# Local attention in 64x32 tiles of the TensorE array instead of 64x64, with queries and keys fetched in another layout

## The chip, the cores and the metric

The kernel runs on one core of a Trainium2 chip. A core has five engines that run their own instruction streams and meet through semaphores: TensorE (PE in the profile; its weight loads are listed apart, as PEld), VectorE (DVE), ScalarE (ACT), GpSimd (POOL) and SyncE (SP), which here does nothing but issue DMAs. TensorE is an array of 128 by 128 cells that can be split into smaller tiles, each with its own stationary operand, its own moving operand and its own place in PSUM. Everything is fp32.

The metric is device time in microseconds of one execution, as the median of several runs. Lower is better.

## The reference

The input is x of 8 batches, 512 tokens, 256 features. It is layer-normed, and two branches start from the result. One is a plain causal attention with one head of 256. The other is a small transformer of two layers, each with local attention and a gated feed-forward part; its output goes through silu and gates the first branch, and x is added. What matters here is the local attention: 8 heads of 64, and windows of 128 queries, each of which sees its own window and the one before.

```python
qkv = h @ wqkv                              # h: tokens, half of the features shifted by one token
q = l2norm(q) * qs;  k = l2norm(k) * ksc
q, k = rotary_xpos(q, k)
# 128 queries (window w) against the 256 keys of windows w-1 and w
sim = jnp.einsum('bhwid,bhwjd->bhwij', bq, bk)
mask = (i < j) | (i > j + WINDOW) | (j == -1)
attn = softmax(where(mask, -max, sim))
out = jnp.einsum('bhwij,bhwjd->bhwid', attn, bv)
x = x + out @ wo
h = layernorm(shift_token(x));  a, g = split(h @ w1 + b1)
x = x + (a * gelu(g)) @ w2 + b2
```

A query with place r in its window may see the keys from place r of the window before to place r of its own: 129 keys.

## The kernel before, in words

The whole program is written as a set of jobs (Python generators), and a string of letters, ORDER, says which job goes on next. A letter stands for a job: A output projections (all_outs), B weighted sums of the values (all_sums), C the attention weights fetched back (p_in), D scores (all_scores), E queries and keys fetched back (turns_in), F the projections to q, k and v, G the late weight loads (late_loads); H and later letters are the first branch, the feed-forward parts and the ends of single batches. TensorE's instructions stand in exactly this order. For the other engines and for SP a planner (class Order) keeps a time line with estimated costs, puts every instruction into the first gap that fits and keeps that order in the program. The planner's estimates are used for the order alone; TensorE, DVE, ACT, POOL and SP each run their instructions strictly one after another, and an instruction that waits holds up those behind it.

The work is done in 16 slots, a slot being one layer of one batch, and in 4 steps t of 128 tokens in each slot: 64 steps. In a step:

- F (project): q, k and v of 128 tokens, three pairs of matmuls of 512 columns on the full array. ACT, DVE and POOL square, rotate and normalise q and k.
- turn_out: q and k are turned by 32x32 blocks on DVE (rt) and sent to DRAM (away) by four DMAs.
- E (turns_in): they come back with features on partitions: k in one DMA (kT, 256 KB), q in four DMAs of 64 KB each (qT), which write pieces of 32 numbers, 128 bytes, so that the 64 queries of a half window lie side by side. There are three buffers for kT, of one step each, and one for qT; a step's keys stay for the next step.
- D (all_scores): for each half g of the heads, 64 queries at a time against the keys that they can see, in tiles of 64 rows (features of one head) by 64 columns (queries); four such tiles fill the array. Two rows of heads (a) times two halves of the window (h) run side by side. The two halves of the window see 192 keys each: 128 in a first matmul and 64 in a second. In step t = 0 there is no window before, and 128 keys are used. DVE adds the mask and takes the greatest (192 columns a head), ACT makes the exponentials and sums, DVE the reciprocals, and either scales.
- p_out: DVE turns the weights by 32x32 blocks (pr), and eight DMAs (four for t = 0) send them to DRAM (p_away).
- C (p_in): two DMAs fetch them back with keys on partitions (pT), three slots of 64 keys.
- B (all_sums): values by weights, in tiles of 64 rows (keys) by 64 columns (features of a head). For each pair of heads (c), matmuls of 128 columns and of 64 columns (queries) write two PSUM banks, which are then added into oT.
- A (all_outs): output projection.

matmul (line 297) tells the planner what a matmul costs: its columns, divided by the number of tiles side by side. `order.CHANGE` holds what the planner reckons for a change of the array's split. All DMAs are issued on SP: load for inputs and weights, send for the rest. late_loads issues the weights of the first layer's feed-forward part and then those of the second layer, a few at a time.

Of the kernel before, what the change touches and what calls it, by code (L numbers as in the profile page):

```python
# [15 lines left out]
P = 128  # L16
BATCH = 8
T = 512
# [11 lines left out]
WINDOW = 128  # L30
EPS = 1e-5
# [11 lines left out]
    "H6JFH2FHFGHF3JHE3NF2HEH3FHFH2FENH2D2HJCE2CJCFJF2EGD2FJGEJ2GEDCDBECEFJC2JFJF2JBEFD2JF2C2E"  # L43
    "GCAEFJ2ABC2FIJFEFEGJ2FJ2GDBDJCN3FENCIAFAI2CNENFIEBDN2FDNIENFNCNIRE2I2C2I3BD2NICEINCFNF3"
    "D2E2NFCAF2EAKNCNBRCNKEKER2CRDRF2BFRDC2AEAFRKDR2EF3EFK2RCF2RDER2CFBEDCDFKRECE2KEKCDBDCFE"
    "F2ACARCRFE2BD2RC2KF2CFLFBCFECK2A2EDLDCEBCECLKF3ELKDF4LRBEDLRF2CE2ACAEFD2FCLECL2D2BFCECFE"
    "FEFCOL2BLACAEDODO2EF2ECFLCF2OEBCDCLF2MFDMECOBEME2FO2CMFD2MAECFAFEO2CBVD2F2C2OFE2FOBFECPF"
    "RC2FD2VAVECEPVFOE2AVPBPC2V2FOPDBFDFEF2CPVDCDCAECEPFVPVFEPFVABDCVEF2CVEFVFDEBFPED2C2E2VPC"
    "PFAF3CFVABE2S2DSCSFPCFPQBDESEQ2FSQCV2CA2D2EC2STVQFEF2ES2DBEDVZSCEFVFCSF2SBD2ZFAEFACFEFST"
    "CE2TCZ2TZ3SBD2C2F2EFCEFZCZBCD2FEFCFAZCTAFZBZTCEFTEZCWEF2TFD2BFCZE2T2ETATAED2WZWFWEWF2CET"  # L50
    "CZ2CTDWBCEDECF4U2CBUFEFWC2WUFA2D2CBCXCUFW2ZFEF3EdWEWZBD2ZECE2FWZCADCDFdAEF2XCWBXdXEdECd2"
    "CFd2EDFBDdEFCXFAXDCDAEFEFCFdECXFX3BCD2aEF3ECdFEXEBD2dCFdF2EdEdXAaC2aCAF2XDFDBC2dadXBEC2E"
    "dEYF2EdECFY2AaADFBDY2bFaC2aFahE2CEFaFaF2BD2CdFEA2aFCECFahbED2b2adhFbCEah2F3D2EBh2Cb2ECEb"
    "FbBDECEC2DFAhCFEAF2BDECDFbEFEeFCbFBbCe2AEACED2eF2ECFCF2bhD2FBC2ebBFECF2AFCECEeEhFEeAFD2C"
    "EBEeCF2ehCEFD2fFEe3EBfD2hCcCF2cAC2AhEfFeBEfCFCeDBDFfFfFC2FE2CcEhEFEA2fDcDf2EF2fFD2CBECh"
    "F2CFfBFCEfEi2FiEFAC2AhiEfBDiDFECF2fCiCDEDciE2i3gi2DBDiCiFCACFAFjgFCjBE2CFCFjFEFBFhA2jE2h"
    "jDhF2DEFhFhD2CgF2jgjC2jEjECEBC2gjED2ECjBCEjFA2l2D2Clj2lkBklC2kl2Cl2klBlA2n2knl2n2m3o2n7o"
    "no"
# [19 lines left out]
class Order:  # L78
# [9 lines left out]
        "full": {"rows": 0.193, "columns": 0.148, "quarters": 0.148},  # L88
        "rows": {"full": 0.196, "columns": 0.142, "quarters": 0.142},
        "columns": {"full": 0.209, "rows": 0.2, "quarters": 0.155},  # L90
        "quarters": {"full": 0.22, "rows": 0.2, "columns": 0.165},
# [150 lines left out]
def gated_attention_kernel(  # L242
# [28 lines left out]
    counts |= {"st": 2, "p0": 2, "p": 6, "pr": 1, "pT": 2, "qT": 1, "kT": 3, "v": 4, "sq": 2, "side": 2}  # L271
# [25 lines left out]
    def matmul(out, lhsT, rhs, start, stop, shape="full"):  # L297
        columns = max(out.free_size(), lhsT.free_size())
        side_by_side = {"full": 1, "rows": 2, "columns": 2, "quarters": 4}[shape]
        order.took((columns * 4 / 2400 * 1.0055 + 0.01 * (shape == "quarters")) / side_by_side, shape)  # L300
        nc.tensor.matmul(out, lhsT=lhsT, rhs=rhs, start=start, stop=stop)  # L301
# [63 lines left out]
    mask_sb = const.tile([P, T + 2 * P], F32, tag="mask", name="mask_sb")  # L365
# [50 lines left out]
    window_mask = mask_sb[:, T + DH : T + 2 * P]  # L416
# [321 lines left out]
    def turns_in():  # L738


        for b, l, t in steps:
            yield {"after": [event("parked", b, l, t)]}
            away, at = parked.pop((b, l, t))
            yield {"free": {"kT": 1}}
            dst = buffer("kT", [P, INNER], f"kT_{b}_{l}_{t}")
            there = send(dst, away[P : 2 * P], at, LAND[256])
            kTs[b, l, t] = dst.rearrange("p (s c b) -> p s c b", s=4, c=IC)
            done("kT", b, l, t, at=there)
            yield {"free": {"qT": 1}}
            dst = buffer("qT", [P, INNER], f"qT_{b}_{l}_{t}")  # L750
            parts = dst.rearrange("p (h c s b) -> h s p c b", h=2, c=IC, s=2)
            for s in range(4):
                src = away[0:P, s * P : (s + 1) * P].rearrange("p (c b) -> p c b", c=IC)
                there = send(parts[s // 2, s % 2], src, at, LAND[64])
            qTs[b, l, t] = dst.rearrange("p (h c n) -> p h c n", h=2, c=IC)
            done("qT", b, l, t, at=there)

    steps = [(b, l, t) for b, l in slots for t in range(NT)]

    def late_loads():  # L760


        yield {"after": [event("asked", 1)]}
        for some in behind_x:
# [21 lines left out]
    main = slice(0, P), slice(P + DH, 2 * P + DH)  # L786
    rest = slice(P, P + DH), slice(2 * P + DH, 3 * P)
    oTs = {}

    def all_scores():  # L790
# [4 lines left out]
        for b, l, t in steps:  # L795
            nm = f"{b}_{l}_{t}"
            n = P if t == 0 else P + DH
            used = main if t == 0 else (slice(0, P + DH), slice(P + DH, 3 * P))
# [4 lines left out]
            for g in range(2):  # L803
# [6 lines left out]
                qT, kT, before = qTs[b, l, t], kTs[b, l, t], kTs.get((b, l, t - 1))  # L810
                sps = [bank(f"sps_{nm}_{g}_{a}") for a in range(2)]
                blocks = [(main, ((before or kT, slice(0, 4)), (kT, slice(0, 4))))]
                if t > 0:
                    blocks.append((rest, ((kT, slice(0, 2)), (before, slice(2, 4)))))
                for columns, keys in blocks:
                    for i in range(2):
                        c = 2 * g + i
                        for a, rows in enumerate(halves):
                            for h, (tile_, some) in enumerate(keys):
                                matmul(  # L820
                                    sps[a][halves[h], columns[i]],
                                    qT[rows, h, c],
                                    tile_[rows, some, c],
                                    True,
                                    True,
                                    "quarters",
                                )
                if g == 1:
                    free(f"qT_{nm}")
                    if t > 0:  # L830
                        free(f"kT_{b}_{l}_{t - 1}")
                    if t == NT - 1:
                        free(f"kT_{nm}")
                ps = []
                for a in range(2):
                    ends = 0.0
                    p = buffer("p", [P, 3 * P], f"p_{nm}_{g}_{a}")
# [42 lines left out]
    def p_out(ps, g, t, key):  # L880
# [5 lines left out]
        few = 4 if t == 0 else 6  # L886
        if g == 0:
            p_leaving[key], there = claimed("pr", [P, 6, HEADS, 32], f"pr_{nm}")
# [3 lines left out]
        for a, (p, at, name) in enumerate(ps):  # L892

            src = p.rearrange("p (h k a) -> p h k a", h=2, k=6)[:, :, 0:few]
# [7 lines left out]
        away = dram.tile([P, 6, 2 * P], F32, tag="p_away", name=f"p_away_{nm}", bufs=8)  # L902
        rows = away.rearrange("(g a) (s q) n -> a g s q n", g=4, q=2)
        for s in range(4):
# [4 lines left out]
            elif s < 2:  # L909
                parts = [((0, 4), 0, 0), ((4, 6), 1, 0)]  # L910
            else:
                parts = [((0, 4), 2, 0), ((4, 6), 1, 2)]
# [6 lines left out]

    p_leaving, pTs = {}, {}  # L920

# [13 lines left out]
    def all_sums():  # L935


        for b, l, t in steps:
# [12 lines left out]
            for c in range(IC):  # L951

                turned = pT[c // 2]
                two = [
                    (halves[a], slice((2 * c + a) * DH, (2 * c + a + 1) * DH), 2 * a + c % 2)
                    for a in range(2)
                ]
                if t == 0:

                    for on, h, to in two:  # L960
                        matmul(o_ps[0][on, c], v[low, h], turned[low, 0:2, :, to], True, True, "quarters")
# [407 lines left out]
```

## Time and profile before

| | |
|---|---|
| median of 3 runs | 1317.12 us (1316.83 to 1318.29) |
| span of the profiled execution | 1320.0 us |
| TensorE (PE) busy | 1292.7 us, 98%, 10498 records |
| weight loads (PEld) busy | 750.0 us, 57% |
| VectorE (DVE) busy | 1030.6 us, 78% |
| ScalarE (ACT) busy | 751.5 us, 57% |
| GpSimd (POOL) busy | 624.5 us, 47% |
| scores, "sps" | 3584 records, 102.2 us busy |
| DMA | 209.49 MB in 396884 packets, mean 159 GB/s |
| packets under 512 bytes | 153880 |

The page gives the profiled execution's span, from the first to the last of its instructions, and no other time of its own. The span is 2.9 us above the median of the runs shown. A record in the profile is one instruction as the engine ran it; an fp32 matmul on the array leaves two records with a weight load each, a transpose one. "Busy" is the union of the records of a group, so that matmuls that run side by side count once, while their mean durations overlap. "Idle before" is time in which the engine had nothing to do ahead of such a record, and the name behind the arrow is what ended it. In names, "sps" are the score banks, "ops" those of the weighted sums, qkv the projections, qT, kT and pT the turned queries, keys and weights, away and p_away the places in DRAM.

### The profile page before, as it was taken

The page shows a single profiled execution, that of the slowest core. Times are in us where ns is not written, and L with a number is a line of the kernel's source. Part 1 is how long each engine was busy: PE and PEld are TensorE (multiplying, and loading weights), DVE is VectorE, ACT ScalarE, POOL GpSimd, SP SyncE. Part 2 cuts the span into 40 slices and gives each one's busy share as a digit, 9 for nine tenths or more (in the row PEclk, how much of TensorE's full clock was granted, in tenths as well). Part 3 has the DMA queues.
Part 4 walks back from the last instruction along what each step waited for, and adds up shares of the span by engine and source line. Part 5 has one row for each costly group of instructions (what it writes and reads, how often), then busy time and mean ns, then how long its engine had stood idle before and what let it go on. Part 6 is the DMA issues. An engine that isn't in the chain of part 4 may idle for free.

```text
span 1320.0 us, 29777 instructions
## 1 busy us (share of the span) xinstructions
PE 1292.7 (98%) x10498; PEld 750.0 (57%) x10498; DVE 1030.6 (78%) x3088; ACT 751.5 (57%) x1958; POOL 624.5 (47%) x651
## 2 busy tenths in 40 slices
PE   9899999999999999999999999999999999999998
PEld 4565565555555565555655555555455555545566
DVE  6977678778778888888777787878878788866864
ACT  2553554754667376574555547655455647662853
POOL 6746336456353644454625445545454644425500
PEclk9999999999999999999999999999999999999999
DMA  7777435765667656666647666566666766645761
GB/s 250 200 189 211 135 94 144 200 150 141 167 164 202 160 131 153 174 162 145 173 104 188 149 156 156 137 181 157 148 152 157 165 159 170 153 113 145 196 165 56
DMA packets 396884, 209.49 MB, mean 159 GB/s; under 512 B 153880, under 2 KB 382400, under 8 KB 396736
## 3 DMA queue, kind: packets, MB, share of 16 engines
q1 hardware_dynamic: 396736, 207.59, 62.1%
q8 instruction: 84, 1.38, 0.4%
q14 instruction: 64, 0.52, 0.1%
HBM read 111.56 MB, written 95.94 MB: 157 GB/s over the span
## 4 chain that ended last, share of the span: by engine, by line
PE 85%; DMA 5%; DVE 3%; SPq 2%; ACT 2%; issue 1%; POOL 1%; DVEq 0%; ACTq 0%; POOLq 0%
PE qkv L301 22%; PE ff L301 20%; PE w2p L301 12%; PE wop L301 7%; PE sps L301 6%; PE ops L301 6%; PE qk L301 3%; SPq L71 2%; PE sc L301 2%; DMA qT<-away 2%; PE av L301 2%; PE v0p L301 2%; PE hps L305 1%; DMA x<-in_x_dram 1%; DMA pT<-p_away 1%
## 5 line engine op out<-in xcount | busy, mean ns | idle before, releaser
L71 POOL TENSOR_TENSOR r<-r,side 128x512 f32<-128x512 f32 x128 | 163.7, 1279 | 428.9 <-DVE side L71 428.6
L301 PE MATMUL qkv<-wqkv,xT 128*128 128x512 f32 x768 | 354.7, 596 | 0.7 <-ACT pT L71 0.7
L301 PE MATMUL ff<-hn,w 128*128 128x512 f32 (+1 forms) x680 | 283.7, 568 | 1.0 <-ACT hn L71 1.0
L71 ACT ACTIVATE p<-p,nmx 128x192 f32<-128x192 f32 (+1 forms) x512 | 219.4, 429 | 83.6 <-DVE nmx L71 82.9
L301 PEld LDWEIGHTS qkv<-wqkv,xT 128*128 128x128 f32 x768 | 141.1, 190 | 142.4 <-issue 129.3
L71 POOL TENSOR_TENSOR rn<-ss,neg_half 128x8 f32<-128x8 f32 x128 | 212.9, 1663 | 10.7
L301 PEld LDWEIGHTS ff<-hn,w 128*128 128x128 f32 x680 | 128.2, 190 | 139.5 <-issue 124.6
L71 DVE CUSTOM_DVE_ANT_0 p<-sps,mask_sb 128x192 f32<-128x192 f32 (+1 forms) x512 | 146.3, 332 | 21.5 <-PE sps L301 21.4
L301 PE MATMUL w2p<-hid,w 128*128 128x512 f32 (+3 forms) x408 | 160.0, 576 | 0.0
L71 ACT ACTIVATE p<-p,rden 128x192 f32<-128x192 f32 (+1 forms) x283 | 118.5, 433 | 40.5 <-DVE rden L71 39.5
L71 DVE STREAM_TRANSPOSE pr<-p 128x384 f32<-128x384 f32 (+1 forms) x256 | 127.7, 526 | 17.8 <-ACT p L71 14.2
L71 POOL TENSOR_TENSOR r<-r,rn 128x512 f32<-128x512 f32 x128 | 133.6, 1044 | 10.0
L71 ACT ACTIVATE sq<-qkv 128x512 f32<-128x512 f32 x128 | 75.0, 592 | 100.0 <-PE qkv L301 90.7
L71 ACT ACT_TABLE_LOAD x99 | 127.0, 1283 | 2.5 <-PEq L1359 0.7
L71 DVE SCALAR_TENSOR_TENSOR hid<-ff,vec,hid 128x512 f32<-128x512 f32 (+3 forms) x119 | 83.3, 711 | 47.5 <-ACT hid L71 26.2
L301 PE MATMUL wop<-oT,wo 128*128 128x256 f32 x512 | 118.6, 380 | 0.5 <-DVE oT L71 0.5
L301 PEld LDWEIGHTS w2p<-hid,w 128*128 128x128 f32 (+1 forms) x408 | 68.8, 189 | 81.2 <-issue 78.3
L71 DVE TENSOR_TENSOR r<-qkv,tables 128x512 f32<-128x512 f32 x128 | 86.9, 679 | 34.3 <-ACT sq L71 29.2
L301 PE MATMUL sps<-kT,qT 64*64 64x128 f32 (+1 forms) x3584 | 102.2, 253 | 10.6 <-DMA qT<-away 10.0
L301 PEld LDWEIGHTS sps<-kT,qT 64*64 64x64 f32 x3584 | 88.3, 135 | 42.2 <-issue 25.4
L301 PEld LDWEIGHTS wop<-oT,wo 128*128 128x128 f32 x512 | 96.0, 190 | 25.6 <-issue 9.3
L71 DVE STREAM_TRANSPOSE rt<-r 128x512 f32<-128x512 f32 x128 | 90.1, 704 | 18.5 <-POOL r L71 14.0
(83 smaller groups left out, 1679.2 us busy)
## 6 DMA issues: line engine op xcount, KB each, us to landing
pT<-p_away SPq DMA_DIRECT2D x96, 384.0 KB, 4.4
away<-rt SPq DMA_DIRECT2D x256, 128.0 KB, 2.6
p_away<-pr SPq DMA_DIRECT2D x256, 128.0 KB, 2.3
kT<-away SPq DMA_DIRECT2D x64, 256.0 KB, 3.0
qT<-away SPq DMA_DIRECT2D x256, 64.0 KB, 2.9
p_away<-pr SPq DMA_DIRECT2D x192, 64.0 KB, 2.0
pT<-p_away SPq DMA_DIRECT2D x32, 256.0 KB, 3.4
hn_away<-hn SPq DMA_DIRECT2D x60, 128.0 KB, 2.5
```

The lines of the kernel that those rows point to most:

```text
L71: ins = getattr(self.engine, name)(*args, **kwargs)
L301: nc.tensor.matmul(out, lhsT=lhsT, rhs=rhs, start=start, stop=stop)
L305: nc.tensor.transpose(out, in_, ident)
```

## The change

Scores: 32 queries instead of 64 per tile. A block of 32 queries sees 160 keys (SEEN), its own block and the four before it, so that one matmul of 160 columns does what took one of 128 and one of 64 for 64 queries. Tiles are 64 rows by 32 columns, eight fill the array. The weights for a head take 160 columns instead of 192 in the mask, the exponentials, the scaling and the turning.

So that the 160 keys lie in one stretch, each kT buffer now holds the keys of the step before and of its own, side by side. For t > 0 the earlier keys are fetched again from DRAM. There are two such buffers instead of three of half the size. The queries come back in one DMA of whole rows.

Sums: the values' matmuls, of the same columns as before, are split into 32 features each, so that they too use 64x32 tiles; there are twice as many. The weights still come back as three slots of 64 keys. Where a block of 32 queries doesn't see a block of 32 keys of its slot, nothing is written any more; those places have to be zero. So the eight DRAM buffers for t > 0 are now fixed ones, taken in turn, and clear_p_aways writes zeros into these places once, with 32 DMAs of 32 rows by 256 numbers, ahead of the first layer's feed-forward weights on SP.

ORDER, the order of all jobs, is a new string throughout (left out below).

```diff
+BLOCK = 32
+SEEN = WINDOW + BLOCK
...
-    counts |= {"st": 2, "p0": 2, "p": 6, "pr": 1, "pT": 2, "qT": 1, "kT": 3, "v": 4, "sq": 2, "side": 2}
+    counts |= {"st": 2, "p0": 2, "p": 6, "pr": 1, "pT": 2, "qT": 1, "kT": 2, "v": 4, "sq": 2, "side": 2}
...
-        side_by_side = {"full": 1, "rows": 2, "columns": 2, "quarters": 4}[shape]
-        order.took((columns * 4 / 2400 * 1.0055 + 0.01 * (shape == "quarters")) / side_by_side, shape)
+        side_by_side = {"full": 1, "rows": 2, "columns": 2, "quarters": 4, "eighths": 8}[shape]
+        order.took((columns * 4 / 2400 * 1.0055 + 0.01 * (side_by_side > 2)) / side_by_side, shape)
...
             yield {"free": {"kT": 1}}
-            dst = buffer("kT", [P, INNER], f"kT_{b}_{l}_{t}")
-            there = send(dst, away[P : 2 * P], at, LAND[256])
-            kTs[b, l, t] = dst.rearrange("p (s c b) -> p s c b", s=4, c=IC)
+            dst = buffer("kT", [P, 2, INNER], f"kT_{b}_{l}_{t}")
+            if t > 0:
+                send(dst[:, 0], keys_of[b, l, t - 1], 0.0, LAND[256])
+            keys_of[b, l, t] = away[P : 2 * P]
+            there = send(dst[:, 1], keys_of[b, l, t], at, LAND[256])
+            kTs[b, l, t] = dst.rearrange("p t (s c b) -> p (t s) c b", s=4, c=IC)
             done("kT", b, l, t, at=there)
             yield {"free": {"qT": 1}}
             dst = buffer("qT", [P, INNER], f"qT_{b}_{l}_{t}")
-            parts = dst.rearrange("p (h c s b) -> h s p c b", h=2, c=IC, s=2)
-            for s in range(4):
-                src = away[0:P, s * P : (s + 1) * P].rearrange("p (c b) -> p c b", c=IC)
-                there = send(parts[s // 2, s % 2], src, at, LAND[64])
-            qTs[b, l, t] = dst.rearrange("p (h c n) -> p h c n", h=2, c=IC)
+            there = send(dst, away[0:P], at, LAND[256])
+            qTs[b, l, t] = dst.rearrange("p (s c b) -> p s c b", s=4, c=IC)
...
         yield {"after": [event("asked", 1)]}
+        clear_p_aways()
         for some in behind_x:
             some()
...
-                blocks = [(main, ((before or kT, slice(0, 4)), (kT, slice(0, 4))))]
-                if t > 0:
-                    blocks.append((rest, ((kT, slice(0, 2)), (before, slice(2, 4)))))
-                for columns, keys in blocks:
-                    for i in range(2):
-                        c = 2 * g + i
-                        for a, rows in enumerate(halves):
-                            for h, (tile_, some) in enumerate(keys):
-                                matmul(
-                                    sps[a][halves[h], columns[i]],
-                                    qT[rows, h, c],
-                                    tile_[rows, some, c],
...
+                for i in range(2):
+                    for a, rows in enumerate(halves):
+                        for q in range(4):
+                            seen = slice(4, 8) if t == 0 else slice(q, q + 5)
+                            matmul(
+                                sps[a][q * BLOCK : (q + 1) * BLOCK, used[i]],
+                                qT[rows, q, 2 * g + i],
+                                kT[rows, seen, 2 * g + i],
+                                True,
+                                True,
+                                "eighths",
+                            )
...
-            elif s < 2:
-                parts = [((0, 4), 0, 0), ((4, 6), 1, 0)]
             else:
-                parts = [((0, 4), 2, 0), ((4, 6), 1, 2)]
+                own = 4 - s
+                parts = [((0, own), s // 2, s), ((own, 5), 1 + s // 2, 0)]
...
+    p_aways = [
+        dram.tile([P, 6, 2 * P], F32, tag=f"p_away{n}", name=f"p_away{n}", bufs=1) for n in range(1, 9)
+    ]
+
+    def clear_p_aways():
+
+        for away in p_aways:
+            for g, slot, q in ((0, 0, 1), (2, 1, 1), (1, 1, 0), (3, 2, 0)):
+                send(rows_of(away)[:, g, slot, q], mask_sb[0:BLOCK, 0 : 2 * P], arrived["mask"], 2.0)
...
-                two = [
-                    (halves[a], slice((2 * c + a) * DH, (2 * c + a + 1) * DH), 2 * a + c % 2)
-                    for a in range(2)
+                four = [
+                    (
+                        slice(n * BLOCK, (n + 1) * BLOCK),
+                        slice(c * P + n * BLOCK, c * P + (n + 1) * BLOCK),
+                        n // 2 * 2 + c % 2,
+                    )
+                    for n in range(4)
                 ]
...
-                for on, h, to in two:
+                for on, h, to in four:
                     for ps, own, tile_, at in ((o_ps[0], low, v, 1), (o_ps[1], up, before, 0)):
                         columns = turned[own, at : at + 2, :, to]
-                        matmul(ps[on, c], tile_[own, h], columns, True, False, "quarters")
-                for on, h, to in two:
+                        matmul(ps[on, c], tile_[own, h], columns, True, False, "eighths")
+                for on, h, to in four:
                     for ps, own, tile_, at in ((o_ps[0], low, before, 0), (o_ps[1], up, v, 2)):
                         columns = turned[own, at, :, to]
-                        matmul(ps[on, c, own], tile_[own, h], columns, False, True, "quarters")
+                        matmul(ps[on, c, own], tile_[own, h], columns, False, True, "eighths")
...
+    row, col = np.arange(P)[:, None] % BLOCK, np.arange(SEEN)[None, :]
+    window = np.where((col >= row) & (col <= row + WINDOW), f(0.0), f(NEG))
```

## The prediction

> **What bounds the kernel now.** First the page's head, the busy shares and the chain that ended last:
>
> ```profile
> span 1320.0 us, 29777 instructions
> ...
> PE 1292.7 (98%) x10498; PEld 750.0 (57%) x10498; DVE 1030.6 (78%) x3088; ACT 751.5 (57%) x1958; POOL 624.5 (47%) x651
> ...
> PE 85%; DMA 5%; DVE 3%; SPq 2%; ACT 2%; issue 1%; POOL 1%; DVEq 0%; ACTq 0%; POOLq 0%
> ```
>
> TensorE has work almost all the time, so only its own time and its few waits can move the end. DVE, at 78%, matters only where TensorE waits for it. So I read TensorE's groups of instructions (shapes kept apart) for the two that change; the columns are records, busy us, mean ns of one, idle us before them:
>
> ```profile
> L301 PE MATMUL ops<-pT,v 64*64 64x128 f32 x1792 | 87.7, 275 | 4.3 <-DMA pT<-p_away 3.5 <-DVE nmx L71 0.8
> L301 PE MATMUL sps<-kT,qT 64*64 64x128 f32 x2048 | 86.8, 277 | 10.6 <-DMA qT<-away 10.0 <-issue 0.2
> L301 PE MATMUL ops<-pT,v 64*64 64x64 f32 x1792 | 70.0, 220 | 0.0
> L301 PE MATMUL sps<-kT,qT 64*64 64x64 f32 x1536 | 43.9, 220 | 0.0
> ```
>
> Means overlap, since four tiles run abreast; costs must come from starts. Each fp32 matmul leaves two records (the program has 1792 of each kind). The timeline of TensorE (start, length, records):
>
> ```profile
> 108.01 0.67 PE L301 MATMUL sps<-kT,qT 64*64 64x128 f32 x16
> ...
> 312.86 1.46 PE L301 MATMUL av<-v,pT 128*128 128x256 f32 x6
> 314.25 1.57 PE L301 MATMUL ops<-pT,v 64*64 64x128 f32 x64
> ...
> 327.93 10.46 PE L301 MATMUL ff<-hn,w 128*128 128x512 f32 x24
> ```
>
> Full array: 24 records of 512 columns give (10.46 - 0.593)/23 = 0.429 us from start to start; 6 of 256 give (1.46 - 0.38)/5 = 0.216. That is 0.83 ns a column plus 3 ns, so 109 ns for 128 columns, 56 for 64 and 136 for 160. Four abreast: "ops" has 32 records of 128 and 32 of 64, 8 rounds of four each: 8 x 109 + 7 x 56 + 220 for the last one + about 70 to get under way = 1.55 us, against 1.57 shown. So a round of four costs what one matmul of its width costs on the full array. In the single records, neighbours in a round start 7 ns apart.
>
> The waits, with the queue (SPq) that serves them; the last line is the median us from issue to landing:
>
> ```profile
> PE sps L301 <- DMA qT<-away: 10.0, 8, 5.8
> ...
> 58.12 0.51 SPq L71 DMA_DIRECT2D wqkv<-in_wqkv_dram  x1
> 58.69 6.38 SPq L71 DMA_DIRECT2D qT<-away  x4
> ...
> qT<-away SPq DMA_DIRECT2D x256, 64.0 KB, 2.9
> ```
>
> TensorE waits 10.0 us for queries in 8 places; 5.8 of it is one wait that ends at 68.5 us, behind the 1.5 MB weight load issued at 58.12.
>
> **The change, part by part.** Durations are from the profiled execution; its span, 1320.0, is all that the page gives of its time, 2.9 us above the median, 1317.12. The sum is a difference, and I take it off the median.
>
> *Scores.* 48 of 64 steps have t > 0. Before, such a step has 8 rounds of 128 columns and 8 of 64: 8 x (109 + 56) = 1.32 us. After, its 32 matmuls leave 64 records of 160 columns, 8 rounds of eight: 8 x 136 = 1.09 us. 48 x 0.23 = **-11.1 us**, if eight run abreast as four do. The 16 steps with t = 0 keep 8 rounds of 128 columns.
>
> *Sums.* The matmuls double (1792 to 3584) and so do the places: 8 rounds of 128 and 8 of 64 a step, **0** by columns. That holds only if twice the instructions can be issued in the same time.
>
> *A round of eight.* No row has one. From below: no dearer than a round of four. From above: in today's 64-column rounds 4 matmuls and 4 weight loads start in 56 ns, 7 ns each; were that the fastest, eight abreast would take 112 ns whatever the width below 128, and a step of sums (8 + 8 rounds) 1.79 instead of 1.32, +22.6 us over 48. After the wait that ends at 324.6, however, pairs of weight load and matmul start 7 ns apart, half of that price, so 8 pairs fit into 56 ns, just. I take 2 ns a round (64-column rounds today stand 56 to 58 apart): 512 rounds of scores and 896 of sums, **+2.8 us** (0 to +22.6). *Stagger:* the eighth tile starts 7 x 7 = 49 ns after the first, the fourth today 21; each stretch of small tiles ends 28 ns later. The order of the changed kernel as built has 99 stretches: **+2.7 us**. *Turning the array:* today there are 94 stretches; going in costs 522 ns where 429 is the rule, coming out 148 instead of 56, so 5 more cost 5 x 0.185 = **+0.9 us**.
>
> [...]
>
> *The transfers.* Queries come in one DMA instead of four, keys in two instead of one: three issues a step, not five, at about 0.5 us each on SP (the row above: 64 KB, 2.9 us; keys 256 KB, 3.0 us). So the last part arrives about 1 us sooner. The keys have two buffers of twice the size, and the next step's are still fetched while this one's are used; the repeated keys have long been in DRAM. The attention weights still leave in eight issues a step with t > 0, with a sixth fewer bytes. Of the seven shorter query waits, 10.0 - 5.8 = 4.2 us, I take half away: **-2** (-4 to +3). The long one stays behind the weight load, but now with about 9 us of TensorE work after the previous scores instead of 8.4, and two issues less: **-2** (-5.8 to +3).
>
> *Clearing.* 32 transfers of 32 KB are put on SP ahead of the first layer's feed-forward weights. At 0.5 us each that is 16 us. SP stands idle from 19.1 to 27.3 and from 27.7 to 31.7 us today, which covers 12, so the first turned keys leave about 4 us late. Today's first queries are issued until 38.4, land 2.9 us later, by about 41, and are used at 44.25; in the new order the scores come 1.4 us sooner (two groups of transposes moved behind). 4 + 1.4 - 3.3 = **+2 us** (0 to +8: 1.9 MB of weights now go just ahead of them in the same queue). What else waits behind the clears, the third batch's input, isn't needed until about 52 us.
>
> *Off the path.* Masks, exponentials, scaling and transposes shrink from 192 to 160 columns a head: 384 masks at 1 ns a column are 13 us less DVE, and ACT loses some 10. Both lie beside TensorE; they only make its waits for DVE and ACT rarer, and I count nothing. The new order of all stages may add or remove single waits; today's waits for anything but queries come to 1320.0 - 1292.7 - 10.0 = 17 us in all, and I allow a quarter of that, 4 us, to either side.
>
> Sum: -11.1 + 2.8 + 2.7 + 0.9 - 2 - 2 + 2 = **-6.7 us**; 1317.1 - 6.7 = 1310.4, faster by 0.5%.
>
> **The rivals.**
> *Only four abreast.* If the array, or what feeds it, carries four streams of fp32 and not eight, every round of eight takes two: +1.09 us for each of 48 steps of scores and +1.32 for sums, and +0.87 for each of 16 first steps in both: 48 x 2.41 + 16 x 1.74 = 143 us, about 1454. For it: no row shows more than two tiles side by side over the same rows. Against: these two cost nothing over one (109 ns both).
> *Issue is the limit (the other side).* In the sums 128 pairs must go out in 1.32 us, 10.3 ns a pair; at 14 ns, today's rate in 64-column rounds, +22.6 instead of +2.8 ends at 1330. It decides from 11.8 ns a pair on, where the sums lose the 9.5 us that the rest of the sum gains. Fetching instructions works alike: queue q8 brings 16 KB packets, 84 of them, which take 0.9 to 1.8 us in the trace and hold 256 instructions each (21500 of TensorE in all); a stretch of sums and scores now takes 384 in 2.4 us, and some 30 stretches could each stand still for up to 0.5 us, +15 us. Against both: 7 ns a pair after a wait.
> *Other waits take the gain.* The early transfers at their upper bound (+8) and the re-made order at +4 give -6.7 + 6 + 4 = +3, so 1315 to 1321. For it: a slow first stage shifts all that follows. Against: TensorE's waits are few.
>
> **How the numbers follow.** Measurement tells from no change what exceeds about 0.2%, 2.6 us. As forecast 0.64 (1302 to 1315, most at 1310; 0.60 of it faster); issue or fetch 0.13 (1317 to 1335); only four, or rounds much longer, 0.10 (1350 up); other waits 0.13 (1312 to 1322; faster 0.03, same 0.05, slower 0.05). Faster 0.63; same 0.04 + 0.05 + 0.01 = 0.10; slower 0.05 + 0.12 + 0.10 = 0.27. The range has to reach into the slower cases: 1301 (waits of DMA nearly gone as well) to 1333; the likeliest case alone is 1302 to 1315.
>
> **What would show it.** Rounds: 64 records of 160-column "sps" in about 1.4 us, 128 records of "ops" in about 1.6; if these stretches are over 2 us, issue or feeding is the limit. Waits: "sps" for queries below 7 us in sum; a wait before the first "sps" near 42 us of about 2 us. Packets of under 512 B fall by the 131072 of 128 bytes. I am wrong if TensorE's starts in a round of eight are not 7 ns apart, or if the feed-forward's first weights come late because of the clears.

## The result, and the profile after

| | before | after |
|---|---|---|
| median | 1317.07 us (1316.83 to 1318.29) | 1357.04 us (1355.24 to 1361.33, 4 runs) |
| ratio | | 1.0304, 95% interval 1.0285 to 1.0322 |
| profiled span | 1320.0 us | 1353.2 us |

The change makes the kernel 3.0% slower; 0.5% faster was forecast, and 1357.04 lies above the upper end of the range, 1333. The page of the changed kernel, the lines that answer to those shown of before:

```profile
span 1353.2 us, 37815 instructions
...
PE 1306.0 (97%) x14594; PEld 746.8 (55%) x14594; DVE 1003.0 (74%) x3085; ACT 741.0 (55%) x1962; POOL 625.5 (46%) x651
...
DMA packets 273267, 217.29 MB, mean 161 GB/s; under 512 B 21016, under 2 KB 244416, under 8 KB 273088
...
q8 instruction: 116, 1.90, 0.6%
...
PE 87%; DMA 6%; DVE 2%; issue 2%; POOL 2%; SPq 1%; ACT 1%; DVEq 0%; ACTq 0%
```

TensorE still bounds the kernel, but it is idle for 47 us of its span and not for 27, and the chain holds 2% of "issue", time in which the engine waited for nothing that the profile shows. While TensorE works, the granted clock is 0.5 for 13.7 us of this trace and for 6.8 us of the one before. A full-array record of 512 columns takes 854 ns from start to start at 0.5 (at 47 us of this trace), where it takes 429 at 1.00, so that is worth at most 3.4 us of the difference. DVE has 28 us less to do, above all as masks and transposes are narrower. Small packets fell by 132864. Instruction packets rose from 84 to 116: 32 more packets of 256 instructions, that is the 8192 that TensorE has more (4096 records with a weight load each).

TensorE's groups by shape, and its waits (waited for, us in all, times, longest):

```profile
L304 PE MATMUL ops<-pT,v 64*32 64x128 f32 x3584 | 104.7, 279 | 3.3 <-DMA pT<-p_away 1.9 <-DVE hid L73 1.2
L304 PE MATMUL ops<-pT,v 64*32 64x64 f32 x3584 | 96.4, 220 | 2.8 <-issue 2.8
L304 PE MATMUL sps<-kT,qT 64*32 64x160 f32 x3072 | 73.5, 304 | 15.4 <-issue 9.1 <-DMA p_away<-pr 3.4 <-DMA qT<-away 2.8
L304 PE MATMUL sps<-kT,qT 64*32 64x128 f32 x1024 | 22.2, 274 | 7.0 <-issue 6.1 <-DMA qT<-away 0.9
```

```profile
PE sps L304 <- issue: 15.3, 12, 2.1
PE pT0p L308 <- ACT p L73: 7.5, 1, 7.5
PE sps L304 <- DMA qT<-away: 3.7, 5, 1.4
...
PE ops L304 <- issue: 2.8, 3, 1.6
```

Three things stand here. The sums' two rows were 87.7 and 70.0 us and are 104.7 and 96.4. Fifteen times TensorE stands still for "issue" in the middle of small tiles, 15.3 + 2.8 = 18.1 us, where before had 0.2. And one wait of 7.5 us is new, ahead of a transpose of the first branch (pT0p). The wait for queries fell from 10.0 to 3.7 us.

TensorE's timeline (start, length, records) shows the two parts of the change side by side, a step of scores alone and a step of sums alone:

```profile
335.06 1.34 PE L304 MATMUL sps<-kT,qT 64*32 64x160 f32 x64
336.33 1.98 PE L304 MATMUL qkv<-wqkv,xT 128*128 128x512 f32 x4
...
1232.97 1.89 PE L304 MATMUL ops<-pT,v 64*32 64x128 f32 x128
1234.78 1.55 PE L304 MATMUL qkv<-wqkv,xT 128*128 128x512 f32 x3
```

and the same two in the kernel before, sums first:

```profile
354.63 1.57 PE L301 MATMUL ops<-pT,v 64*64 64x128 f32 x64
356.13 1.97 PE L301 MATMUL ff<-hn,tail 128*106 128x512 f32 x4
...
361.48 1.57 PE L301 MATMUL sps<-kT,qT 64*64 64x128 f32 x64
362.98 1.09 PE L305 MATMUL hps<-ident,xT 128*128 128x128 f32 x8
```

From the first start to that of the work behind it, the scores take 336.33 - 335.06 = 1.27 us and took 362.98 - 361.48 = 1.50: 0.23 less, as the prediction had it for the columns. The sums take 1.81 and took 356.13 - 354.63 = 1.50: 0.31 more, where 0 was forecast. These steps are typical: by the single records, the median of all such steps that stand alone and have no wait inside went from 1.50 to 1.27 us for scores (18 and 20 steps) and from 1.50 to 1.82 for sums (17 and 16).

In the single records of the step at 1232.97, the first 32 matmul records start 6.7 ns apart within a round, and the rounds keep the pace of the columns; from the 33rd to the 128th the mean from start to start is 13.9 ns. By the medians over such steps, 16 records of 128 columns then take 15 to 19 ns each and 16 of 64 columns 10 to 13, where the columns, eight abreast, would give 13.6 and 7. In the scores a round of eight takes 136 ns from the second on, 17 ns a record.

### The profile page after: what moved, and what is told of

Same layout as the page of the kernel before. It is cut to its first block, busy times and chain, and to the rows that moved or that the text cites. A ratio compares the mean times of both kernels' runs of the same rounds, so it can differ in the third digit from the quotient of the medians.

```text
span 1353.2 us, 37815 instructions
## 1 busy us (share of the span) xinstructions
PE 1306.0 (97%) x14594; PEld 746.8 (55%) x14594; DVE 1003.0 (74%) x3085; ACT 741.0 (55%) x1962; POOL 625.5 (46%) x651
## 4 chain that ended last, share of the span: by engine, by line
PE 87%; DMA 6%; DVE 2%; issue 2%; POOL 2%; SPq 1%; ACT 1%; DVEq 0%; ACTq 0%
PE qkv L304 22%; PE ff L304 21%; PE w2p L304 11%; PE wop L304 8%; PE ops L304 7%; PE sps L304 6%; PE qk L304 3%; PE av L304 2%; DMA qT<-away 2%; PE sc L304 2%; DMA x<-in_x_dram 1%; PE v0p L304 1%; PE hps L308 1%; POOL r L73 1%; SPq L73 1%
## 5 line engine op out<-in xcount | busy, mean ns | idle before, releaser
L304 PE MATMUL qkv<-wqkv,xT 128*128 128x512 f32 x768 | 359.4, 600 | 0.6 <-DVE side L73 0.6
L73 ACT ACTIVATE p<-p,nmx 128x160 f32<-128x160 f32 (+1 forms) x512 | 209.2, 410 | 69.4 <-DVE nmx L73 68.5
L73 POOL TENSOR_TENSOR rn<-ss,neg_half 128x8 f32<-128x8 f32 x128 | 213.4, 1667 | 10.7
L73 DVE CUSTOM_DVE_ANT_0 p<-sps,mask_sb 128x160 f32<-128x160 f32 (+1 forms) x512 | 134.2, 307 | 21.5 <-PE sps L304 21.4
L73 ACT ACTIVATE p<-p,rden 128x160 f32<-128x160 f32 (+1 forms) x279 | 112.4, 414 | 45.1 <-DVE rden L73 44.3
L73 DVE STREAM_TRANSPOSE pr<-p 128x320 f32<-128x320 f32 (+1 forms) x256 | 116.1, 478 | 18.9 <-ACT p L73 12.7
L304 PEld LDWEIGHTS ops<-pT,v 64*32 64x32 f32 x7168 | 99.6, 106 | 36.7 <-issue 22.8
L304 PE MATMUL sps<-kT,qT 64*32 64x160 f32 (+1 forms) x4096 | 95.7, 296 | 22.5 <-issue 15.3
L304 PE MATMUL ops<-pT,v 64*32 64x128 f32 (+1 forms) x7168 | 111.2, 249 | 6.0 <-issue 2.8
L304 PEld LDWEIGHTS wop<-oT,wo 128*128 128x128 f32 x512 | 96.7, 190 | 29.5 <-issue 13.9
```

The lines of the kernel that those rows point to most:

```text
L73: ins = getattr(self.engine, name)(*args, **kwargs)
```

## The experiments

Each timed kernel was compared with runs of the kernel before on the same chip; since the chip is another from one group of runs to the next (the kernel before had medians of 1315.77 to 1317.68 us on them), ratios compare better than times. Three theories stood against each other. A: TensorE is not given its instructions fast enough. B: the early transfers and the new order make the waits. C: the array runs slower with eight tiles than with four.

### Sums back in 64x64, clears moved, both

The first run undoes the sums alone (the scores, the clears and the new order stay); the planner is told the cost that it had:

```diff
-                for on, h, to in four:
+                for on, h, to in two:
                     for ps, own, tile_, at in ((o_ps[0], low, v, 1), (o_ps[1], up, before, 0)):
                         columns = turned[own, at : at + 2, :, to]
-                        matmul(ps[on, c], tile_[own, h], columns, True, False, "eighths")
+                        matmul(ps[on, c], tile_[own, h], columns, True, False, "eighths", 4)
```

> The changed kernel with the weighted sums alone put back into 64x64 tiles (1792 matmuls instead of 3584); scores stay in 64x32 tiles, the order of all engines is kept. Theory A, instructions: TensorE's instructions cannot be issued and fetched as fast as eight tiles use them up; then a stretch of sums alone goes back from 1.82 to about 1.50 us, the waits of 1.2 to 2.3 us inside stretches (some 21 us in sum, released by nothing that the profile shows) go almost entirely, and the time falls by 25 to 35 us, to 1322 to 1332. Theory B, the early transfers and the new order: nothing of that is touched, so at most 5 us, and the waits inside the scores stay. Theory C, the array is slower when eight streams are read: the sums alone get faster by 0.3 us a step, 15 us, but the waits inside the scores stay, so about 1342.

Measured: 1318.65 us, ratio 1.0015 (1.0000 to 1.0031). One edit takes back 38.4 of the 40 us, 3 us more than A had expected at best. The second run leaves the sums and sends the clears of a buffer just before its first use:

```diff
-        clear_p_aways()
         for some in behind_x:
...
             p_aways.append(away)
+            if len(cleared) < 8:
+                cleared.append(away)
+                clear_p_away(away)
```

> The changed kernel with each of the eight DRAM buffers cleared just before its first use (4 transfers at a time, over the first eight steps) instead of all 32 transfers ahead of the feed-forward weights. Theory B: the wait of 7.7 us that ends at 47.5 us and what follows from it go, 10 us or more, to 1345 or less. Theory A: the wait at 47.5 us may go, but the waits inside the stretches stay as they are; not below 1345.

Measured: 1359.09 us, ratio 1.0320 (1.0293 to 1.0347): no gain, though the wait of 7.5 us ahead of pT0p shrank to 0.8. Both edits together:

> Both: sums back in 64x64 tiles and the clears spread; scores in 64x32 tiles are then what is left of the change. If A and B are both right and independent: 1312 to 1322, level with the kernel before or just under it (scores 11 us less; some 37 more changes between 64x64 and 64x32 tiles at 0.1 to 0.2 us each, 4 to 7 us more).

Measured: 1318.88 us, ratio 1.0014 (1.0001 to 1.0028). B's part is not the clears at this place; the loss is in the sums.

### The sums' tiles alone, in the kernel before

The opposite edit: the kernel before, its order and its scores, and only the values' matmuls split into 64x32, with the planner's cost as it was.

```diff
-                for on, h, to in two:
+                for on, h, to in four:
                     for ps, own, tile_, at in ((o_ps[0], low, v, 1), (o_ps[1], up, before, 0)):
                         columns = turned[own, at : at + 2, :, to]
-                        matmul(ps[on, c], tile_[own, h], columns, True, False, "quarters")
+                        matmul(ps[on, c], tile_[own, h], columns, True, False, "quarters", 8)
```

> The kernel before with the weighted sums alone in 64x32 tiles (3584 matmuls instead of 1792); scores, transfers, clears and the order of all engines as before. Theory A (instructions): a stretch of sums alone goes from 1.50 to about 1.82 us, stretches of sums and scores stand still for 1 to 2 us where the next packet of instructions isn't there, and the kernel gets slower by 30 to 45 us, to 1347 to 1362. Theory B (transfers, order): nothing of that is in this kernel, so 1317 to 1325 (some 45 more changes of the tile size cost a few us).

Measured: 1359.13 us, ratio 1.0315 (1.0296 to 1.0334). A row of its timeline and two of its waits:

```profile
324.64 1.89 PE L303 MATMUL ops<-pT,v 64*32 64x128 f32 x128
```

```profile
PE ops L303 <- issue: 8.6, 5, 2.3
PE sps L303 <- issue: 3.8, 4, 1.4
```

The same 1.89 us for a step of sums, and standstills for issue (12.4 us; before has 0.2), also ahead of its untouched 64x64 scores. The doubling alone costs 41 us, in a kernel that has neither the new order nor the new transfers nor the clears. C as it stands is wrong, since eight tiles side by side, 160 columns wide, take 136 ns a round, what the columns take; what they do with fewer columns is seen below.

### Where in a stretch TensorE stands still

A stretch of 128 records of sums and 64 of scores in the changed kernel, and the same stretch with the sums in 64x64 (the first run above):

```profile
470.74 1.89 PE L304 MATMUL ops<-pT,v 64*32 64x128 f32 x128
472.50 0.77 PE L304 MATMUL sps<-kT,qT 64*32 64x160 f32 x30
475.00 1.00 PE L304 MATMUL sps<-kT,qT 64*32 64x160 f32 x34 [1.74 <-issue]
475.93 1.98 PE L304 MATMUL qkv<-wqkv,xT 128*128 128x512 f32 x4
```

```profile
462.36 1.57 PE L305 MATMUL ops<-pT,v 64*64 64x128 f32 x64
463.86 1.34 PE L305 MATMUL sps<-kT,qT 64*32 64x160 f32 x64
465.13 1.98 PE L305 MATMUL qkv<-wqkv,xT 128*128 128x512 f32 x4
```

5.19 us against 2.77. In the first, 128 + 30 records with a weight load each, 316 instructions, run off; then TensorE stands for 1.74 us in the midst of the scores, with queries and keys long there. At each of the fifteen standstills of the changed kernel a packet of the instruction queue q8 had ended 1.2 to 1.7 us before TensorE went on. To see whether that follows the number of instructions, four long stretches of small tiles on zeros were put in front of the kernel before (extra work, so its time says nothing):

```diff
+        abreast(256, 64, 64)
+        abreast(512, 32, 64)
+        abreast(256, 32, 160)
+        abreast(512, 32, 128)
```

(matmuls, columns of the tile, columns of the moving operand; in all four the tiles have 64 rows, and take turns over the whole array.)

> The kernel before, with four stretches of extra matmuls on a tile of zeros in front, each followed by 8 matmuls of the full array: 256 of 64 columns in 64x64 tiles, 512 of 64 columns in 64x32, 256 of 160 columns in 64x32, 512 of 128 columns in 64x32. Their columns alone would take 7.2, 7.2, 8.7 and 14 us. They are 1024, 2048, 1024 and 2048 instructions, that is 4, 8, 4 and 8 packets of 256. Theory A: all are limited by instructions, with rounds at full speed and standstills between them at every 256 instructions; at one packet in about 2.5 us the stretches take 8 to 10, 18 to 22, 9 to 11 and 18 to 22 us, the 64-column one in 64x32 no faster than the 128-column one. Theory C (eight streams slow the array down): no standstills, rounds stretched evenly, and the stretch in 64x64 tiles takes its 7.2 us. The time of the kernel itself isn't compared.

The starts after five of the seven standstills in the last stretch, and what queue q8 brought from the first of these lines to 109.43 us, six standstills in all:

```profile
88.72 0.31 PE L1275 MATMUL idle_other<-idle 64*32 64x128 f32 x4 [0.93 <-issue]
92.17 0.31 PE L1275 MATMUL idle_other<-idle 64*32 64x128 f32 x4 [1.44 <-issue]
95.62 0.31 PE L1275 MATMUL idle_other<-idle 64*32 64x128 f32 x4 [1.44 <-issue]
99.08 0.31 PE L1275 MATMUL idle_other<-idle 64*32 64x128 f32 x4 [1.44 <-issue]
102.53 0.31 PE L1275 MATMUL idle_other<-idle 64*32 64x128 f32 x4 [1.44 <-issue]
```

```profile
q8 instruction: 6, 0.10, 1.8%
```

Every 3.45 us, and between two standstills exactly 128 records, 256 instructions, one packet of 16 KB. They run off in 1.75 us, 13.8 ns a record, and then TensorE stands for 1.71 us from the last start to the next. A packet starts about 1.1 us after TensorE went on, takes 0.92 to 1.23 us of the queue, and ends 1.2 to 1.5 us before TensorE goes on again; what happens ahead of it and behind it no view shows. The first standstill of the three 64x32 stretches came after 169 to 201 records, 338 to 402 instructions: so much lies ready at the start. The standstills are where A put them, but longer than it had reckoned: the four stretches took 17.0, 26.3, 12.4 and 26.0 us.

Between standstills the pace has to be read with the granted clock, which was 1.00 from 30.5 to 36.6 us, 0.50 from there to 60.5 and 1.00 for the last two stretches. Eight abreast at 1.00, a round took 133 ns with 160 columns and 110 with 128, what the columns take (136 and 109). With 64 columns it took 78 ns (9.8 a record, 329 records), where the columns take 56. At 0.50 the same round took 109 ns, about twice the 56. Four abreast with 64 columns took 59 ns at 1.00. So rounds of eight with 64 columns didn't run at the columns' pace even with the instructions at hand. Of the sums, six of the eight 64-column rounds of a step lie behind its first 32 records, and 6 x 22 ns is 0.13 of the 0.32 us. The rest, in a step that mixes both widths, was not explained, nor did a run tell whether the weight loads or the issuing of instructions sets the 9.8 ns.

### Sums and scores kept apart

The changed kernel with its instructions, in an order in which a group of full-array matmuls is moved between sums and scores wherever one could be found, such as, in a piece of the string written out (B sums, D scores, K a feed-forward part):

```diff
-FLDBDFCEFCKLK
+FLDKBDFCEFCLK
```

> The changed kernel, all of it, with the same instructions, in an order in which the sums of one step and the scores of another hardly ever follow one another directly: in the changed kernel 41 of 99 stretches of small tiles hold both, here 11 of 135, because a group of full-array matmuls has been moved between them. If TensorE is short of instructions (theory A), a stretch of 320 to 384 instructions outruns what has been brought, and one of 256 hardly does: the idle time put down to issue ahead of sps and ops, 18.5 us in the changed kernel, falls below 8, 36 more turns of the array cost 7 us, and the time is 1341 to 1351. If the doubled sums cost the array itself a fixed time for each matmul, or each stretch, nothing is gained by this and the 36 more turns cost 7 to 13 us: 1362 to 1372.

Measured: 1352.3 us, ratio 1.0273 (1.0256 to 1.0291). The waits for issue, and the step of sums that stood in the stretch above:

```profile
PE sps L304 <- issue: 5.1, 4, 2.0
...
PE ops L304 <- issue: 2.3, 2, 1.2
```

```profile
474.16 1.89 PE L304 MATMUL ops<-pT,v 64*32 64x128 f32 x128
475.98 1.98 PE L304 MATMUL qk<-xT,wa 128*128 128x512 f32 x4
477.89 1.34 PE L304 MATMUL sps<-kT,qT 64*32 64x160 f32 x64
479.16 1.12 PE L304 MATMUL qkv<-wqkv,xT 128*128 128x512 f32 x2
```

Standing still for issue fell from 18.1 to 7.4 us, as A expected; 1.82 + 1.27 us take the place of 5.19. The time missed A's bound by 1 us and the rival's by 10. The 36 further turns of the array, at the prediction's 0.185 us, eat 6.7 of the 10.7 us, and the intervals of the two ratios still touch: the standstills follow the length of the stretch, but this is no way to win them back.

### The order and the clears

What is left of the forecast gain with the sums undone? The changed kernel with the order of before, first with the sums as changed:

> The changed kernel with the string ORDER of the kernel before. Theory A: sums and scores adjoin in the old order too, so the waits inside the stretches stay, 1340 to 1360. If instead the new order of the jobs is what costs, the time goes below 1330.

Measured: 1365.28 us, ratio 1.0370 (1.0351 to 1.0390), above what was expected; the wait ahead of pT0p is 15.7 us there. The other three have the sums in 64x64 (the last of them is the very first run with the order of before). In two of them the first buffer is cleared at the start, each further one on SP behind the step that wrote the one before it:

```diff
-        clear_p_aways()
+        clear_p_away(p_aways[0])
...
         gone(f"pr_{nm}", there)
+        if t > 0 and len(cleared) < 8:
+            cleared.append(p_aways[0])
+            clear_p_away(p_aways[0])
```

> As e1 (sums in 64x64, scores in 64x32 tiles), but only the first DRAM buffer is cleared at the start, and each of the next seven right behind the step that wrote the one before it, off the way of the weights that are just leaving. If the clears ahead of the third batch's input cause the 7.7 us wait at 47.5 us, it goes, and nothing as long comes in its place as it did with clears just before use: 1308 to 1314, faster than the kernel before. If the waits of the first 100 us only move, it stays at 1317 to 1320.

> As e7 with the string ORDER of the kernel before: 94 stretches of small tiles instead of 99 and the old sequence of jobs, which was made for other lengths. 1308 to 1320; below e7 if the number of stretches counts, above it if the new order fits the shorter scores better.

> Scores alone in 64x32, sums in 64x64, all clears ahead of the feed-forward weights as in the changed kernel, and the order of before: the fourth corner beside the same with the new order (1318.65), with clears behind the writes and the new order (1317.9) and with clears behind and the old order (1311.3). If the clears hold up the third batch's input and the old order has nothing to put beside that (the wait for p ahead of pT0p was 15.9 us long in the changed kernel with the old order), this ends at 1319 to 1327, and the clears are worth 8 to 16 us in the old order though nothing in the new one. If the gain of the corner at 1311.3 is the old order's alone, wherever the clears stand, it ends at 1310 to 1314.

Scores alone in 64x32, four corners, us and ratio to before:

| | new order | order of before |
|---|---|---|
| clears ahead of the weights | 1318.65, 1.0015 (1.0000 to 1.0031) | 1327.92, 1.0091 (1.0070 to 1.0112) |
| clears behind the writes | 1317.93, 1.0001 (0.9991 to 1.0011) | 1311.30, 0.9959 (0.9944 to 0.9973) |

So the scores' tiles alone, in the old order, reach the time that was forecast for the whole, 1311.3 where 1310.4 was said. That the numbers agree is in part luck, since the terms differ: between the two traces (spans 1320.0 and 1309.4) TensorE is busy 4.6 us less and idle 6.0 us less. The clears ahead of the weights cost 16.6 us in the old order, just above what was expected, and 0.7 in the new one. Part of the 16.6 is the clock: it is granted at 0.5 for 30.7 us of the trace with the clears ahead and for 13.7 us of the one with them behind. Where the time goes is seen on DVE, before and after (in front the third batch's input on SP, before and after):

```profile
27.27 0.40 SPq L71 DMA_DIRECT2D x<-in_x_dram  x1
...
32.25 1.39 DVE L71 BATCH_NORM_STATS2 stats_x<-x 128x6 f32<-128x256 f32 x4
```

```profile
16.59 15.20 SPq L73 DMA_DIRECT2D p_away<-mask_sb  x28
...
36.17 0.56 SPq L73 DMA_DIRECT2D x<-in_x_dram  x1
...
42.73 1.41 DVE L73 BATCH_NORM_STATS2 stats_x<-x 128x6 f32<-128x256 f32 x4 [10.62 <-DMA x<-in_x_dram]
...
47.50 0.90 PE L308 MATMUL pT0p<-ident,p 128*128 128x128 f32 x3 [7.55 <-ACT p L73]
```

The clears hold SP for 15.2 us, the input is issued at 36.17 and not at 27.27, and the statistics that need it stand on DVE ahead of the mask of the first branch's scores, on which ACT's exponential and TensorE's transposes wait. In the new order the clears' wait could be taken away (0.8 us left with the clears behind), but two waits of 3.5 us for the attention weights came in at 68 and 86 us; in the old order the removal was pure gain. Whether the new order is slower in itself was asked with it in the kernel before:

> The kernel before, with the changed kernel's order and nothing else. With scores in 64x32 and clears behind, the new order was 6.6 us slower than the old one. If that is what the new order costs by itself, this ends at 1321 to 1326. If the new order is as good as the old one where there are no clears, it ends at 1315 to 1319.

Measured: 1341.03 us, ratio 1.0191 (1.0162 to 1.0220), worse than either expectation; the wait for queries rose from 10.0 to 15.0 us, and that for the weights from 3.5 to 5.5. The order was made for one DMA for the queries and not four, and the two waits that grew are waits for DMAs, so this run may not give the new order's own price; their 7 us are not all of the 25. Why the new order lost 6.6 us against the old one with the clears behind stays open: beside its two waits of 3.5 us the old one has a wait of 8.0 us of its own.

### A better version

In the corner at 1311.3 one long wait was left at 70.74 us: the scores' queries were issued behind the load of the second layer's projection weights. That load was moved behind them in the order (the second G of this piece, a late load, past the eight letters behind it):

```diff
-FFEGDDFJGEJJGEDCDBE
+FFEGDDFJEJJGEDCDGBE
```

> The version with scores alone in 64x32, clears behind the writes and the order of before; only the load of the second layer's projection weights (1.5 MB) goes to SP after the queries of the third step and the writes that follow them, and no longer ahead of them. In the version without this the scores of that step wait 8.0 us until 70.7 us. If that wait is the load's, 3 to 5 us of it go and the time is 1306 to 1309; if it is the clears' or the writes' that surround it, it stays at 1310 to 1312.

The corner at 1311.3, then this version; SP's queue, and TensorE's start of the scores:

```profile
62.48 0.39 SPq L73 DMA_DIRECT2D wqkv<-in_wqkv_dram  x1
63.87 0.34 SPq L73 DMA_DIRECT2D qT<-away  x1
...
70.74 2.48 PE L305 MATMUL sps<-kT,qT 64*32 64x160 f32 x64 [8.04 <-DMA p_away<-pr]
```

```profile
62.48 0.34 SPq L73 DMA_DIRECT2D qT<-away  x1
...
67.08 0.44 SPq L73 DMA_DIRECT2D wqkv<-in_wqkv_dram  x1
...
66.13 2.48 PE L305 MATMUL sps<-kT,qT 64*32 64x160 f32 x64 [3.41 <-DMA qT<-away]
```

Measured: 1307.74 us (1305.48 to 1311.38, 6 runs), ratio 0.9939 (0.9921 to 0.9957), the best of all versions. In the trace the scores start 4.6 us sooner, and the time is 3.6 us lower: most of the wait was the load's. By the ratios, which allow for the chips, the gain over that corner is 0.2% and the two intervals overlap; against the kernel before, the gain is clear. The profile named the attention weights' DMAs as the first wait's releaser; with the load out of the way, the second shows that the queries were waited for.

## Why the prediction was wrong, point by point

- **Scores, -11.1 us: right by the step.** 1.50 to 1.27 us a step of 64 records that stands alone, eight abreast at 136 ns a round. With the sums in 64x64, all stretches of small tiles together lost 173.8 - 186.4 = -12.6 us (first start to the next full-array start, 99 and 94 stretches, from the single records); 5.8 of it are shorter waits inside them, which were 6.9 us and are 1.1. Where sums in 64x64 stand just ahead of scores in 64x32, less was won: both together took 2.84 us before and 2.69 to 2.77 then, where 0.23 less would be 2.61; in the other sequence it was 2.61.
- **Sums, 0 by columns, and a round of eight at +2.8: this is the step that failed.** It said that 0 "holds only if twice the instructions can be issued in the same time", and took for proof that pairs after a wait start 7 ns apart. That pace holds within the rounds of the first 32 pairs of a step of sums; a step has 128, and from then on a record takes 13.9 ns in the mean, the 64-column ones 10 to 13 instead of 7. Even the long stretch on zeros needed 78 ns for a round of eight with 64 columns, where 56 and 2 were reckoned. 48 x 0.32 = 15 us were measured for the steps, between the 0 that was taken and the upper end of +22.6 that stood beside it.
- **Fetching, "up to 0.5 us" in some 30 stretches, +15, inside a rival of 0.13.** The mechanism was named and its size was off: a standstill is 1.2 us in the mean and 2.1 at most in the changed kernel, since 256 instructions come every 3.45 us and not in the 0.9 to 1.8 that the packet occupies its queue. Stretches with the sums doubled cost 210.2 - 173.8 = 36.4 us more: 18 us standstills, most of the rest slower rounds. Both halves of the rival "issue is the limit" came at once, where it counted either; its 1330 was too low for that reason, though its name for the slower rounds, issue, is not shown against the weight loads.
- **Only four abreast: refuted** by the 136 ns rounds of the scores, in each of which four tiles stand side by side over the same rows.
- **Stagger and turns, +2.7 and +0.9:** the stagger of 28 ns doesn't show in the scores. A step that stands alone takes 0.18 us beyond its rounds, before (1.50 - 1.32) and after (1.27 - 1.09). The turns were not told apart from the rest by any run.
- **Transfers, -2 and -2: right in sign, larger.** Waits for queries fell from 10.0 to 3.7 us, none of them longer than 1.4; how much of it is the single DMA and how much the new order was not told apart.
- **Clearing, +2 (0 to +8): wrong in its cover.** "Isn't needed until about 52 us" looked at TensorE; DVE reads that input at 32.25 us in the trace of before, in a fixed place of its order. The price is 16.6 us in the old order, the lower clock behind the wait included; in the new one moving the clears gained 0.7 us, as other waits came in.
- **Off the path, 0: right.** DVE's 28 us less (13 had been said, for the masks alone) bought nothing that a run shows.
- **Other waits:** without the sums the change as made is a rival's case, 1315 to 1321: measured 1318.65.

## What to carry to other kernels

Count instructions per microsecond, not columns alone: in these runs splitting matmuls over more tiles paid where a round of eight took as long as its columns (136 ns at 160 columns), and lost where it did not (78 ns and more at 64 columns, for 56 by columns). Read the sustained pace from the middle of a long stretch, never from its first instructions (6.7 ns a record there and 13.9 behind them), look at the granted clock beside it (109 ns a round at 0.50, 78 at 1.00), and compare the instructions of a whole stretch with what lies ready, here 316 to 402 of TensorE's, before you place two such stretches next to each other. Price a bulk of cheap DMAs on one queue by the first consumer behind it in every engine's order, not only in TensorE's: here it was DVE that waited, 10.6 us, and the kernel lost 16.6 in the old order.

## What the runs showed of the hardware beyond that

- Eight fp32 tiles of 64x32 with 160 columns run together at 136 ns a round in the changed kernel. By 0.83 ns a column and 3 ns, worked out from 429 ns at 512 columns and 216 at 256, one matmul of 160 columns on the full array would take as much; that is an estimate, since no run has one.
- TensorE starts a matmul record with its weight load every 6.7 ns within a round, for the first 32 records of a step of sums, and every 13.9 ns in the mean from then on. In a long stretch of 64x32 tiles with 64 columns it was 9.8 ns at a granted clock of 1.00 and 13.6 at 0.50.
- In a steady run TensorE gets 256 instructions in 3.45 us, 13.5 ns each, at a granted clock of 1.00. At 0.50 for all but the first 6 us, 2048 instructions took 26.3 us, where they took 26.0 at 1.00. A full-array matmul record of 512 columns and its weight load take 429 ns, so nothing of this shows in most of the kernel.
